# Pairwise outer-product batch norm: row 19's scale and shift spread by themselves, two pairs of its first tile done on VectorE alone, and another share for GpSimd in tiles 3 to 10

## The chip, the cores and the metric

The kernel runs on one core of one Trainium2 chip. The metric is the device time of one execution in microseconds (us); lower is better. Below, ACT is ScalarE, DVE is VectorE, POOL is GpSimd, PE is TensorE and SP is SyncE, as in the profile. SP only issues DMAs here.

## What is computed

There are 1024 samples, each with two tables of 39 rows of 16 numbers, `r_xi` and `r_xj`. For each of the 741 pairs (row r, column c < r) the kernel forms the 16x16 outer product of `xj[r]` and `xi[c]`, normalises each pair over all samples and all 256 elements, applies gamma and beta, and multiplies by a 16x16 weight.

```python
rows, cols = np.tril_indices(39, k=-1)
cross = xj[:, rows, :, None] * xi[:, cols, None, :]          # 1024 x 741 x 16 x 16
mean = jnp.mean(cross, axis=(0, 2, 3), keepdims=True)
var = jnp.mean(jnp.square(cross - mean), axis=(0, 2, 3), keepdims=True)
normed = (cross - mean) * jax.lax.rsqrt(var + 1e-5)
normed = normed * gamma[None, :, None, None] + beta[None, :, None, None]
out = normed[:, :, None, :, :] * W[None, None, :, :, :]      # 1024 x 1 x 741 x 16 x 16, f32
```

The inputs are 5 MB, the output is 777 MB. All arithmetic is f32.

## The kernel before

**Statistics first.** The 1024 samples lie as 128 partitions x 8 (index `t`). The means and variances of all pairs come from sums and small matmuls over the inputs, never from the products. This takes the first 33 us. At its end `stq` holds, for a table of 39x39 pairs, a scale s and a shift t. A matmul for each row against `pick` (line 473) spreads the s and t of that row to all 128 partitions, into PSUM. `ROW_GROUPS` (line 32) says which rows are spread together and which PSUM bank they go to: row 19 is group 0, in a bank of its own; row 20 is group 1 and rows 15 to 18 are group 2, and these two share a bank. `apply(group)` (lines 486 to 493, on DVE) multiplies in gamma and beta and leaves s and t in `st_sb`. From then on a pair is one affine step and one multiplication by the weight W.

**Tiles.** A tile is one row r with two of the eight `t` (T = 2), so r pairs of 2x256 elements, which is 0.26 MB a pair over the 128 partitions. The list of tiles begins with row 19 four times (tiles n = 0 to 3), then goes on with rows 20 and 18 in turn (n = 4 to 11), then 21 and 17, and so on. Counted from one, as in the words of the change, tiles 3 to 10 are n = 2 to 9. The output tile lies in `y_sb`, a ring which holds about four tiles; a tile's place is free again when the store of the tile that was there has landed.

**A tile from n = 1 on** goes through these steps, all written out in program order for each engine:

- `scale_xi(n)` (line 166): POOL writes `xs`, the xi rows times s. There are two buffers for `xs`, so `scale_xi(n + 2)` has to wait until ACT and POOL have finished `products(n)`.
- `products(n)` (lines 144 and 146): 2 x 16 instructions, one for each `t` and each i, which multiply `xs` by one element of xj. ACT does i < `split`, POOL the others: POOL has `POOL_I_FIRST` = 6 of 16 for n = 1 and 2, and `POOL_I` = 4 later on.
- `finish(n)`: y = (y + t) x W. DVE does it in one instruction for each pair (line 277). POOL does the last pairs of the tile, with one instruction for each pair (line 263) and one multiplication by W for all of them (line 266); their number is `int(r * 0.13 + 0.5)`, which is 2 for rows 18 and 19 and 3 for row 20.
- `store` (line 208): SP issues one DMA for each piece. The pieces of the first eight tiles are in `FIRST_PIECES`; for n = 2 they end at pairs 4, 11 and 19, for n = 3 at 9 and 19. From n = 8 to the tiles of row 24 a tile is one piece. SP issues in program order, so a piece that is not ready holds those behind it.

In the loop, POOL's order is `scale_xi(n + 2)`, its part of `finish(n)`, its part of `products(n + 1)`. DVE's is `finish(n)`, then an `apply` at n = 2, 4, 8, 16 and 24.

**Tile n = 0** is different. Its products are made without s while the statistics are still being computed (`raw_products`). When `apply(0)` is done, `affine` does y = y x s + t for each pair, the even pairs on ACT (line 221) and the odd ones on POOL (line 223), and `weigh` (line 231) multiplies a piece by W on DVE and stores it. The pieces end at pairs 2, 5, 9, 14 and 19. DVE's order is `apply(0)`, `apply(1)`, `weigh(0)`, `finish(1)`. POOL's order is five of its pairs, `scale_xi(1)`, the other four, `products(1)`, `scale_xi(2)`, and then the loop.

**Tile n = 1** (`RAW`) is finished separately for each of its two `t`, 19 pairs each, with pieces ending at pairs 4, 9, 14 and 19.

Of the kernel before, what the change touches and what calls it, by code (L numbers as in the profile page):

```python
# [9 lines left out]
ALU = mybir.AluOpType  # L10
# [6 lines left out]

ONE, LONG = 24, 33
FIRST_PIECES = (
    (0, 2, 5, 9, 14, 19), (0, 4, 9, 14, 19), (0, 4, 11, 19), (0, 9, 19), (0, 10, 20), (0, 9, 18), (0, 10, 20), (0, 9, 18)  # L20
)


POOL_I, POOL_I_LONG, POOL_I_FIRST = 4, 5, 6
POOL_SHARE, POOL_PAIRS_LONG = 0.13, 8

LOADS = (1, 2, 3, 4, 6, 8)

SHORT = 4


ROW_GROUPS = (
    (19, 20, 0, None), (20, 21, 1, None), (15, 19, 1, 2), (21, 25, 2, 4), (1, 15, 2, 8), (25, 32, 3, 16), (32, 39, 4, 24)
)


@with_exitstack
def tile_pair_outer_batchnorm(
# [15 lines left out]
    nc = tc.nc  # L54
    P = nc.NUM_PARTITIONS
    NB, F, E = xi.shape
# [8 lines left out]
    mid = (F - 1) // 2  # L65
    tiles = [(mid, t0, t0 // T * half // 2) for t0 in range(0, NT, T)]
# [8 lines left out]
    RAW = 1  # L75
# [58 lines left out]
    def view(n):  # L134
        r, _, u = tiles[n]
        return y_sb[:, u : u + T * r, :].rearrange("p (t n) e -> p t n e", t=T)

    def product(n, engine, t, i, src):

        r, t0, _ = tiles[n]  # L140
        y = view(n).rearrange("p t n (i j) -> p t n i j", j=E)[:, t, :, i, :]
        scale = xj_sb[:, t0 + t, r, i : i + 1]
        if engine is nc.scalar:
            nc.scalar.activation(y, src, AF.Copy, scale=scale)  # L144
        else:
            engine.tensor_scalar(y, src, scale, 1.0, ALU.mult, ALU.mult)  # L146
# [13 lines left out]
    def scale_xi(n):  # L160
        r, t0, _ = tiles[n]
        if r <= SHORT:
            return
        n0 = first[r]
        xs = scaled.tile([P, T, r, E], F32, tag="xs", name=f"xs_{r}_{t0}")
        nc.gpsimd.tensor_tensor(  # L166
            xs,
            xi_sb[:, t0 : t0 + T, 0:r, :],
            s_sb[:, :, n0 : n0 + r, :].to_broadcast([P, T, r, E]),
            ALU.mult,  # L170
        )
        xs_of[n] = xs

    def products(n):

        r, t0, _ = tiles[n]
        if r <= SHORT:
            xs = scaled_short.tile([P, T, r, E], F32, tag="xs_short", name=f"xs_{r}_{t0}")
            nc.vector.tensor_tensor(  # L179
                xs,  # L180
                xi_sb[:, t0 : t0 + T, 0:r, :],
                s_short[:, first[r] : first[r] + r]
                .unsqueeze(1)
                .unsqueeze(3)
                .to_broadcast([P, T, r, E]),
                ALU.mult,
            )
            for t in range(T):
                nc.vector.tensor_tensor(  # L189
                    view(n)[:, t].rearrange("p n (i j) -> p n i j", j=E),  # L190
                    xs[:, t].unsqueeze(2).to_broadcast([P, r, E, E]),
                    xj_short[:, t0 + t, r - 1 : r, :].unsqueeze(3).to_broadcast([P, r, E, E]),
                    ALU.mult,
                )
            return
        xs = xs_of.pop(n)
        split = E - (POOL_I_FIRST if n < 3 else POOL_I_LONG if tiles[n][0] > LONG else POOL_I)
        for t in range(T):
            for i in range(E):
                product(n, nc.scalar if i < split else nc.gpsimd, t, i, xs[:, t])  # L200
# [9 lines left out]
                view(n)[:, t : t + step, c0:c1, :].rearrange("p t n e -> p t (n e)"),  # L210
            )

    def affine(n, pairs):

        r = tiles[n][0]
        y = view(n)
        for c in pairs:
            s_c = st_sb[:, 0, first[r] + c : first[r] + c + 1]
            t_c = t_sb[:, first[r] + c : first[r] + c + 1]
            if c % 2 == 0:  # L220
                nc.scalar.activation(y[:, :, c, :], y[:, :, c, :], AF.Identity, bias=t_c, scale=s_c)  # L221
            else:
                nc.gpsimd.tensor_scalar(  # L223
                    y[:, :, c, :], y[:, :, c, :], s_c, t_c, ALU.mult, ALU.add
                )

    def weigh(n):

        y = view(n)
        for c0, c1 in zip(bounds(n), bounds(n)[1:]):  # L230
            nc.vector.tensor_tensor(  # L231
                y[:, :, c0:c1, :],
                y[:, :, c0:c1, :],
                w_dve.unsqueeze(1).to_broadcast([P, T, c1 - c0, EE]),
                ALU.mult,
            )
            store(n, c0, c1)

    def bounds(n):
        if n < len(FIRST_PIECES):  # L240
            return FIRST_PIECES[n]
        r = tiles[n][0]
        pieces = 1 + (r > ONE)
        return tuple(q * r // pieces for q in range(pieces + 1))

    def finish(n):


        r = tiles[n][0]
        n0 = first[r]  # L250
        y = view(n)
        long = r > LONG
        p1 = r // 2 if long else r
        p0 = p1 - (POOL_PAIRS_LONG if long else int(r * POOL_SHARE + 0.5) if r > SHORT else 0)
        step = POOL_PAIRS_LONG // 2 if long else r
        for c0 in range(p0, p1, step):
            c1 = min(c0 + step, p1)
            for c in range(c0, c1):
                t_c = t_sb[:, n0 + c : n0 + c + 1]
                if long:  # L260
                    nc.scalar.activation(y[:, :, c, :], y[:, :, c, :], AF.Identity, bias=t_c)  # L261
                else:
                    nc.gpsimd.tensor_scalar(  # L263
                        y[:, :, c, :], y[:, :, c, :], t_c, 1.0, ALU.add, ALU.mult
                    )
            nc.gpsimd.tensor_tensor(  # L266
                y[:, :, c0:c1, :],
                y[:, :, c0:c1, :],
                w_sb.unsqueeze(1).to_broadcast([P, T, c1 - c0, EE]),
                ALU.mult,  # L270
            )

        size = 1 if n == RAW else T
        for t in range(0, T, size):
            for c0, c1 in zip(bounds(n), bounds(n)[1:]):
                for c in [*range(c0, min(c1, p0)), *range(max(c0, p1), c1)]:
                    stt(  # L277
                        y[:, t : t + size, c, :],
                        y[:, t : t + size, c, :],
                        t_sb[:, n0 + c : n0 + c + 1],  # L280
                        w_dve.to_broadcast([P, size, EE]),
                        ALU.add,
                        ALU.mult,
                    )
                store(n, c0, c1, t, t + size)

    with tc.manual_schedule():
# [176 lines left out]

        spread_of = []
        used = [0] * len(ps_st)
        for r0, r1, bank, _ in ROW_GROUPS:
            n0, n1 = first[r0], first[r1 - 1] + r1 - 1
            at = used[bank]
            used[bank] = at + 2 * (n1 - n0)  # L470
            ps = ps_st[bank][:, at : used[bank]].rearrange("p (x n) -> p x n", x=2)
            for r in range(r0, r1):
                nc.tensor.matmul(  # L473
                    ps[:, :, first[r] - n0 : first[r] - n0 + r],
                    pick[:, r, :],
                    stq[:, :, 0:r],
                    start=True,
                    stop=True,
                )
            spread_of.append((ps, n0, n1))  # L480
            if r0 == 1:
                s_short = ps[:, 0]

        def apply(group):
            ps, n0, n1 = spread_of[group]
            nc.vector.tensor_mul(ps[:, 1], ps[:, 1], st_sb[:, 0, n0:n1])
            if n0 == 0:

                nc.vector.tensor_mul(ps[:, 0], ps[:, 0], st_sb[:, 0, n0:n1])
                nc.vector.tensor_copy(st_sb[:, 0, n0:n1], ps[:, 0])  # L490
            else:
                nc.vector.tensor_mul(st_sb[:, 0, n0:n1], ps[:, 0], st_sb[:, 0, n0:n1])
            nc.vector.tensor_add(st_sb[:, 1, n0:n1], ps[:, 1], st_sb[:, 1, n0:n1])

        apply(0)
        apply(1)

        affine(0, range(0, 11))
        scale_xi(1)
        affine(0, range(11, mid))  # L500
        weigh(0)
        products(1)
        scale_xi(2)

        for n in range(1, len(tiles)):
            if n + 2 < len(tiles):
                scale_xi(n + 2)
            finish(n)
            for group, (_, _, _, tile_of) in enumerate(ROW_GROUPS):
                if n == tile_of:  # L510
                    apply(group)
            if n + 1 < len(tiles):
                products(n + 1)
            if n == 32:
                nc.scalar.copy(xj_short, xj_sb[:, :, 1 : SHORT + 1, :])

# [27 lines left out]
```

## Time and profile before

| what | value |
|---|---|
| time, median of 4 runs | 1883.93 us (1883.58 to 1884.62) |
| the profiled execution: its own time | 1883.58 us |
| the profiled execution: span from first to last instruction | 1881.9 us |
| DVE, ACT, POOL busy | 92%, 87%, 81% of the span |
| output written | 776.99 MB |
| DMA queue of the stores (q1), share of the 16 DMA engines' span | 98.2% |

Times inside the execution are counted from the first instruction. The difference of 1.7 us between the span and the execution's own time lies outside the span. A row of the timeline merges like instructions that follow each other on one engine: start, duration, engine, line, result and operands, and how many; in square brackets stands the idle time of the engine before it and what ended it. A row of the windows view gives, for one stretch of the span, the busy time of each engine, then the granted TensorE clock, the mean busy share of the 16 DMA engines and the rate that they moved.

### The profile page before, as it was taken

To read this page: it belongs to the slowest core of one execution; us is meant where nothing else is said; L and a number is where in the kernel's file an instruction comes from. 1 tells how busy PE (TensorE), PEld (TensorE's weight loads), DVE (VectorE), ACT (ScalarE), POOL (GpSimd) and SP (SyncE) were. 2 spreads that over 40 slices of the span, in tenths; PEclk is the share of its full clock that TensorE was granted. 3 is DMA by queue.
4 is the path that set the end of the run, shared out by engine and by line. 5 is a ranking of instruction groups with operands and counts; after the bars stand their busy time and mean duration, and the time that the engine had idled before them with its cause. 6 is when DMAs were issued, how large, how long until landed. Compare 5 with 4: busy or idle time off the path is not lost. (4 is left out here: it accounts for less than half of the span.)

```text
span 1881.9 us, 9653 instructions
## 1 busy us (share of the span) xinstructions
PE 26.0 (1%) x130; PEld 23.3 (1%) x130; DVE 1721.9 (92%) x2627; ACT 1642.8 (87%) x3415; POOL 1524.6 (81%) x1744
## 2 busy tenths in 40 slices
PE   5000000000000000000000000000000000000000
PEld 4000000000000000000000000000000000000000
DVE  7999999998989898989898989898999999988885
ACT  8998989898989798989898989898988888888883
POOL 8998878787888787878787878787888787777873
DMA  5999999999999999999999999999999999999999
GB/s 197 374 412 427 427 430 426 431 425 425 425 427 424 427 423 424 425 424 424 426 424 423 425 426 423 418 424 423 420 422 425 423 423 426 419 423 414 425 418 410
DMA packets 63722, 783.63 MB, mean 416 GB/s; under 512 B 4768, under 2 KB 6176, under 8 KB 16800
## 3 DMA queue, kind: packets, MB, share of 16 engines
q1 hardware_dynamic: 62352, 779.72, 98.2%
q10 hardware_dynamic: 1296, 3.29, 0.5%
q14 instruction: 73, 0.60, 0.1%
q8 instruction: 1, 0.02, 0.0%
HBM read 6.00 MB, written 776.99 MB: 416 GB/s over the span
## 5 line engine op out<-in xcount | busy, mean ns | idle before, releaser
L277 DVE SCALAR_TENSOR_TENSOR y_sb<-y_sb,st_sb,w_dve 128x512 f32<-128x512 f32 (+1 forms) x2516 | 1654.2, 737 | 131.6 <-issue 118.3
L144 ACT ACTIVATE y_sb<-xs,xj_sb 128x288 f32<-128x288 f32 (+21 forms) x3192 | 1510.0, 568 | 195.2 <-DMA out_dram<-y_sb 168.7
L146 POOL TENSOR_SCALAR y_sb<-xs,xj_sb 128x384 f32<-128x384 f32 (+27 forms) x1128 | 605.7, 560 | 44.3 <-DMA out_dram<-y_sb 25.4
L266 POOL TENSOR_TENSOR y_sb<-y_sb,w_sb 128x2048 f32<-128x2048 f32 (+3 forms) x155 | 511.8, 3308 | 104.0 <-ACT y_sb L261 94.4
L166 POOL TENSOR_TENSOR xs<-xi_sb,st_sb 128x640 f32<-128x640 f32 (+33 forms) x135 | 184.0, 1363 | 177.6 <-ACT y_sb L144 172.8
L263 POOL TENSOR_SCALAR y_sb<-y_sb,st_sb 128x512 f32<-128x512 f32 x286 | 193.5, 692 | 0.1
L261 ACT ACTIVATE y_sb<-y_sb,st_sb 128x512 f32<-128x512 f32 x160 | 100.2, 708 | 1.9
L189 DVE TENSOR_TENSOR y_sb<-xs,ps 128x1024 f32<-128x1024 f32 (+3 forms) x32 | 24.8, 817 | 0.6
L473 PE MATMUL ps<-y_sb 39*128 39x38 f32 (+37 forms) x76 | 16.5, 398 | 2.8 <-DVE y_sb L461 2.8
L473 PEld LDWEIGHTS ps<-y_sb 39*128 39x128 f32 x76 | 16.3, 330 | 3.1 <-DVE y_sb L461 3.1
L339 ACT ACTIVATE y_sb<-y_sb 128x1248 f32<-128x1248 f32 x8 | 9.9, 1244 | 2.8 <-POOL y_sb L328 2.5
L344 DVE TENSOR_REDUCE y_sb<-y_sb 128x78 f32<-128x1248 f32 x8 | 11.2, 1445 | 0.4 <-ACT y_sb L339 0.4
L144 ACT ACTIVATE y_sb<-xi_sb,xj_sb 128x304 f32<-128x304 f32 x24 | 11.4, 537 | 0.0
L328 POOL TENSOR_TENSOR y_sb<-xi_sb,y_sb 128x1248 f32<-128x1248 f32 x4 | 9.2, 2323 | 2.2 <-ACT y_sb L377 2.2
L231 DVE TENSOR_TENSOR y_sb<-y_sb,w_dve 128x2560 f32<-128x2560 f32 (+3 forms) x5 | 10.5, 2170 | 0.0
L318 DVE TENSOR_REDUCE y_sb<-xi_sb 128x39 f32<-128x624 f32 (+1 forms) x6 | 6.1, 1011 | 3.9 <-DMA xi_sb<-in_r_xi_dram 3.9
L328 POOL TENSOR_TENSOR y_sb<-xj_sb,y_sb 128x1248 f32<-128x1248 f32 x4 | 9.2, 2317 | 0.0
L223 POOL TENSOR_SCALAR y_sb<-y_sb,st_sb 128x512 f32<-128x512 f32 x9 | 6.8, 766 | 2.1 <-ACT y_sb L144 2.1
L364 PE MATMUL ps<-y_sb 128*39 128x79 f32 x48 | 8.1, 340 | 15.2 <-DVE y_sb L344 15.1
L221 ACT ACTIVATE y_sb<-y_sb,st_sb 128x512 f32<-128x512 f32 x10 | 7.2, 800 | 0.2 <-ACT y_sb L144 0.2
L318 DVE TENSOR_REDUCE y_sb<-xj_sb 128x39 f32<-128x624 f32 (+1 forms) x6 | 6.1, 1014 | 0.6 <-DMA xj_sb<-in_r_xj_dram 0.6
L364 PEld LDWEIGHTS ps<-y_sb 128*39 128x39 f32 x48 | 5.8, 177 | 17.3 <-DVE y_sb L344 10.6
(58 smaller groups left out, 33.6 us busy)
## 6 DMA issues: line engine op xcount, KB each, us to landing
out_dram<-y_sb SPq DMA_DIRECT2D x25, 2304.0 KB, 14.6
out_dram<-y_sb SPq DMA_DIRECT2D x12, 4352.0 KB, 15.4
out_dram<-y_sb SPq DMA_DIRECT2D x12, 4096.0 KB, 16.3
out_dram<-y_sb SPq DMA_DIRECT2D x10, 4608.0 KB, 14.7
out_dram<-y_sb SPq DMA_DIRECT2D x12, 3840.0 KB, 17.5
out_dram<-y_sb SPq DMA_DIRECT2D x21, 2048.0 KB, 17.0
out_dram<-y_sb SPq DMA_DIRECT2D x12, 3584.0 KB, 18.1
out_dram<-y_sb SPq DMA_DIRECT2D x12, 3328.0 KB, 18.1
```

What stands on the lines that cost most here:

```text
L144: nc.scalar.activation(y, src, AF.Copy, scale=scale)
L146: engine.tensor_scalar(y, src, scale, 1.0, ALU.mult, ALU.mult)
L166: nc.gpsimd.tensor_tensor(xs, xi_sb[:, t0 : t0 + T, 0:r, :], s_sb[:, :, n0 : n0 + r, :].to_broadcast([P, T, r, E]), ALU.mult,)
L189: nc.vector.tensor_tensor(view(n)[:, t].rearrange("p n (i j) -> p n i j", j=E), xs[:, t].unsqueeze(2).to_broadcast([P, r, E, E]), xj_short ...
L261: nc.scalar.activation(y[:, :, c, :], y[:, :, c, :], AF.Identity, bias=t_c)
L263: nc.gpsimd.tensor_scalar(y[:, :, c, :], y[:, :, c, :], t_c, 1.0, ALU.add, ALU.mult)
L266: nc.gpsimd.tensor_tensor(y[:, :, c0:c1, :], y[:, :, c0:c1, :], w_sb.unsqueeze(1).to_broadcast([P, T, c1 - c0, EE]), ALU.mult,)
L277: stt(y[:, t : t + size, c, :], y[:, t : t + size, c, :], t_sb[:, n0 + c : n0 + c + 1], w_dve.to_broadcast([P, size, EE]), ALU.add, ALU.mult,)
L318: nc.vector.tensor_reduce(total[:, t0:t1, part(x)], sources[x][:, t0:t1], AX.X, ALU.add)
L328: nc.gpsimd.tensor_tensor(devs[n % 7], sources[x][:, t0 : t0 + T], shift[:, x : x + 1, :].unsqueeze(3).to_broadcast([P, T, F, E]), ALU.sub ...
L364: nc.tensor.matmul(ps_g[acc][0:F, 0 : 2 * F + 1], lhs, fb[:, t], start=t == 0, stop=t == NT - 1)
L473: nc.tensor.matmul(ps[:, :, first[r] - n0 : first[r] - n0 + r], pick[:, r, :], stq[:, :, 0:r], start=True, stop=True,)
```

## The change

- Only row 19's spread is issued before `apply(0)`. The spreads of the other groups come later in the program, after `weigh(0)`, and `apply(1)` with them. On PE the order of the matmuls is unchanged.
- In tile 0, pairs 0 and 1 (`OWN` = 2) get their affine step on DVE, inside `weigh`, ahead of the piece that they belong to. ACT and POOL begin with pairs 2 and 3, and ACT has nine pairs instead of ten, POOL eight instead of nine.
- Tile 0's pieces now end at pairs 1, 3, 6, 10, 14 and 19: six instead of five, the first of a single pair.
- `POOL_I_FIRST` becomes (6, 6, 5): in `products(2)` POOL has 5 of 16 and ACT 11. (The entry for n = 0 is not used.)
- In `finish(n)` for n = 2 to 9 POOL has three pairs. That is one more than before for n = 2, 3, 5, 7 and 9 (rows 19 and 18) and the same as before for row 20.

```diff
-    (0, 2, 5, 9, 14, 19), (0, 4, 9, 14, 19), (0, 4, 11, 19), (0, 9, 19), ...
+    (0, 1, 3, 6, 10, 14, 19), (0, 4, 9, 14, 19), (0, 4, 11, 19), (0, 9, 19), ...
-POOL_I, POOL_I_LONG, POOL_I_FIRST = 4, 5, 6
-POOL_SHARE, POOL_PAIRS_LONG = 0.13, 8
+POOL_I, POOL_I_LONG, POOL_I_FIRST = 4, 5, (6, 6, 5)
+POOL_SHARE, POOL_PAIRS_LONG, POOL_PAIRS_FIRST = 0.13, 8, 3
-SHORT = 4
+SHORT, OWN = 4, 2
...
-        split = E - (POOL_I_FIRST if n < 3 else POOL_I_LONG if tiles[n][0] > LONG else POOL_I)
+        split = E - (POOL_I_FIRST[n] if n < 3 else POOL_I_LONG if tiles[n][0] > LONG else POOL_I)
...
-    def affine(n, pairs):
+    def affine(n, pairs, engines=(nc.scalar, nc.gpsimd)):
...
-            if c % 2 == 0:
+            engine = engines[c % len(engines)]
+            if engine is nc.scalar:
                 nc.scalar.activation(y[:, :, c, :], y[:, :, c, :], AF.Identity, bias=t_c, scale=s_c)
             else:
-                nc.gpsimd.tensor_scalar(
-                    y[:, :, c, :], y[:, :, c, :], s_c, t_c, ALU.mult, ALU.add
-                )
+                engine.tensor_scalar(y[:, :, c, :], y[:, :, c, :], s_c, t_c, ALU.mult, ALU.add)
 
     def weigh(n):
...
         for c0, c1 in zip(bounds(n), bounds(n)[1:]):
+            affine(n, range(c0, min(c1, OWN)), (nc.vector,))
             nc.vector.tensor_tensor(
...
-        p0 = p1 - (POOL_PAIRS_LONG if long else int(r * POOL_SHARE + 0.5) if r > SHORT else 0)
+        if long:
+            share = POOL_PAIRS_LONG
+        elif RAW < n < 10:
+            share = POOL_PAIRS_FIRST
+        else:
+            share = int(r * POOL_SHARE + 0.5) if r > SHORT else 0
+        p0 = p1 - share
...
+        spread(0)
         apply(0)
+
+        affine(0, range(OWN, 12))
+        scale_xi(1)
+        affine(0, range(12, mid))
+        weigh(0)
+        for group in range(1, len(ROW_GROUPS)):
+            spread(group)
+        s_short = spread_of[SHORT_GROUP][0][:, 0]
         apply(1)
-
-        affine(0, range(0, 11))
-        scale_xi(1)
-        affine(0, range(11, mid))
-        weigh(0)
         products(1)
         scale_xi(2)
```

More of the change, by code (lines that the diff above doesn't have):

```diff
@@ L19 @@
 FIRST_PIECES = (
-    (0, 2, 5, 9, 14, 19), (0, 4, 9, 14, 19), (0, 4, 11, 19), (0, 9, 19), (0, 10, 20), (0, 9, 18), (0, 10, 20), (0, 9, 18)
+    (0, 1, 3, 6, 10, 14, 19), (0, 4, 9, 14, 19), (0, 4, 11, 19), (0, 9, 19), (0, 10, 20), (0, 9, 18), (0, 10, 20), (0, 9, 18)
 )
-POOL_I, POOL_I_LONG, POOL_I_FIRST = 4, 5, 6
-POOL_SHARE, POOL_PAIRS_LONG = 0.13, 8
+POOL_I, POOL_I_LONG, POOL_I_FIRST = 4, 5, (6, 6, 5)
+POOL_SHARE, POOL_PAIRS_LONG, POOL_PAIRS_FIRST = 0.13, 8, 3
 LOADS = (1, 2, 3, 4, 6, 8)
-SHORT = 4
+SHORT, OWN = 4, 2
 ROW_GROUPS = (
@@ L34 @@
 )
+SHORT_GROUP = 4
 @with_exitstack
@@ L466, in tile_pair_outer_batchnorm, with spread @@
         used = [0] * len(ps_st)
-        for r0, r1, bank, _ in ROW_GROUPS:
+        def spread(group):
+            r0, r1, bank, _ = ROW_GROUPS[group]
             n0, n1 = first[r0], first[r1 - 1] + r1 - 1
@@ L480, in tile_pair_outer_batchnorm @@
             spread_of.append((ps, n0, n1))
-            if r0 == 1:
-                s_short = ps[:, 0]
         def apply(group):
@@ L486, in apply @@
             nc.vector.tensor_mul(ps[:, 1], ps[:, 1], st_sb[:, 0, n0:n1])
-            if n0 == 0:
+            if group == SHORT_GROUP:
                 nc.vector.tensor_mul(ps[:, 0], ps[:, 0], st_sb[:, 0, n0:n1])
```

## The prediction

> **What bounds the kernel now.** First the page's DMA rows: from the third slice on the 16 DMA engines are 90% busy or more at about 425 GB/s. 777 MB at that rate take nearly the whole span, so the time is: when the stores begin, plus their length, plus the stretches in which the DMA engines have nothing to move.
>
> ```profile
> DMA  5999999999999999999999999999999999999999
> q1 hardware_dynamic: 62352, 779.72, 98.2%
> ```
>
> Second, the windows view (last two columns: DMA share, GB/s) finds those stretches.
>
> ```profile
> 38.00:39.00 1.00, 1.00 (x6) 1.00 (x7) 1.00 (x1) 1.00 (x3) 1.00 (x2) 1.00 0.58 207
> 55.00:57.00 2.00, 0.00 (x0) 0.00 (x0) 2.00 (x7) 2.00 (x6) 2.00 (x5) 1.00 0.81 325
> 64.20:65.20 1.00, 0.00 (x0) 0.00 (x0) 1.00 (x2) 1.00 (x4) 1.00 (x1) 1.00 0.01 4
> 67.80:69.70 1.90, 0.00 (x0) 0.00 (x0) 1.90 (x4) 1.90 (x6) 1.90 (x5) 1.00 0.05 19
> 79.20:80.20 1.00, 0.00 (x0) 0.00 (x0) 1.00 (x2) 1.00 (x3) 1.00 (x3) 1.00 0.00 0
> 80.20:139.20 59.00, 0.00 (x0) 0.00 (x0) 58.97 (x93) 59.00 (x136) 57.20 (x74) 1.00 1.01 422
> 139.20:140.70 1.50, 0.00 (x0) 0.00 (x0) 1.43 (x6) 1.50 (x5) 1.50 (x4) 1.00 0.11 43
> 200.00:1881.00 1681.00, 0.00 (x0) 0.00 (x0) 1533.26 (x2330) 1460.06 (x3012) 1348.71 (x1521) 1.00 1.00 424
> ```
>
> After the stores begin at 38.4, idle times are 0.4 (55 to 57), 1.0, 1.8, 1.0 and, at 139.2, 1.3 us, 5.5 in all. After 140.7 the queue stays fed. Meanwhile DVE, ACT and POOL are all full: compute is what the DMA waits for until 140.7, and not after it.
>
> Third, the timeline says which engine that is.
>
> ```profile
> 33.74 0.18 DVE L486 TENSOR_TENSOR ps<-ps,st_sb 128x19 f32<-128x19 f32 x1 [0.73 <-PE ps L473]
> 35.87 0.19 DVE L486 TENSOR_TENSOR ps<-ps,st_sb 128x20 f32<-128x20 f32 x1 [1.65 <-PE ps L473]
> 36.27 10.53 DVE L231 TENSOR_TENSOR y_sb<-y_sb,w_dve 128x1024 f32<-128x1024 f32 x5
> 46.73 13.40 DVE L277 SCALAR_TENSOR_TENSOR y_sb<-y_sb,st_sb,w_dve 128x256 f32<-128x256 f32 x34
> 61.43 11.28 DVE L277 SCALAR_TENSOR_TENSOR y_sb<-y_sb,st_sb,w_dve 128x512 f32<-128x512 f32 x17 [1.30 <-POOL y_sb L146]
> 34.38 7.16 ACT L221 ACTIVATE y_sb<-y_sb,st_sb 128x512 f32<-128x512 f32 x10 [0.17 <-ACT y_sb L144]
> 50.47 1.23 POOL L166 TENSOR_TENSOR xs<-xi_sb,st_sb 128x608 f32<-128x608 f32 x1 [0.95 <-ACT y_sb L144]
> 55.45 5.94 POOL L146 TENSOR_SCALAR y_sb<-xs,xj_sb 128x304 f32<-128x304 f32 x12
> 73.29 1.17 POOL L166 TENSOR_TENSOR xs<-xi_sb,st_sb 128x576 f32<-128x576 f32 x1 [2.81 <-ACT y_sb L144]
> 85.74 3.44 POOL L266 TENSOR_TENSOR y_sb<-y_sb,w_sb 128x1536 f32<-128x1536 f32 x1
> 64.30 4.87 SPq L208 DMA_DIRECT2D out_dram<-y_sb  x2
> 139.83 0.37 SPq L208 DMA_DIRECT2D out_dram<-y_sb  x1
> ```
>
> `apply(1)` holds DVE 1.65 us before its first weighing: rows 20 and 15 to 18 share a bank. At 61.43 DVE waits for POOL's half of tile 2. A store's data begin 0.9 us after its issue (64.30 to 65.2; 139.83 to 140.7). POOL at 73.29 really waits for row 18's scale, which `apply(2)` leaves at 73.25; ACT had long been done.
>
> **The change, step by step.** *Tile 0, DVE.* `apply(0)` ends at 34.22; the 1.65 us wait is gone, since `apply(1)` now follows `weigh(0)` and the matmuls are done by then. DVE's `affine` is an instruction that this trace does not show. The nearest row is DVE's own line 277 on 128x512: 11.28 / 17 = 0.66 us. Its smallest rows (0.17) are the floor; the ceiling is 0.75, one line 277 alone, plus up to 0.76 for the second one if it must wait for a POOL `affine` (POOL has one every 0.75 there). Two of them: 0.34 to 2.26; I take 1.32. Line 231 took 1.21 for two pairs and 1.74 for three, so 0.67 for one: pair 0 is weighed at 34.3 + 0.66 + 0.67 = 35.65, stored at 35.7 instead of 37.51. First store 1.8 us earlier. All of `weigh`: before 36.27 to 46.73; now 34.3 + 1.32 + 10.46 + 0.1 (one more instruction) = 46.2, with `apply(1)` (0.4) 46.6. `finish(1)` thus begins 0.1 earlier and, at 13.40, ends at 60.0. The ACT and POOL pairs that `weigh` needs are all there earlier, so they cost nothing.
>
> Here the Trainium skill's VectorE: DVE Perf Modes, section "The perf-mode tier table", gives f32 `tensor_scalar` in SBUF two elements a cycle; an estimate from its clock and its fixed 150 cycles is 0.42 us, and by it the sum would gain 0.25 more. Its SBUF — State Buffer, section "SBUF: two separate sides", speaks against the change: such an instruction and a GpSimd one block each other, because the port pair is an exclusive lock. No row before shows this; the wait it would bring is inside my ceiling.
>
> *Tile 1 and 2, ACT and POOL.* ACT has one `affine` less: 7.16 / 10, so 0.71 earlier. It then frees `xs` 0.71 earlier, and POOL's 50.47 becomes 49.76 (POOL's own chain, one `affine` of 0.75 shorter, has 0.95 of slack there, which covers a lock). POOL's `products(2)` begins at 54.74 and has 10 instead of 12 instructions of 5.94 / 12 = 0.495: done at 59.7. ACT has 22 instead of 20 at 0.44: 59.0 - 0.71 + 0.88 + 0.1 = 59.3. So `finish(2)` begins at 60.0, set by DVE, not at 61.43.
>
> *Tile 2 on DVE.* 16 pairs instead of 17: 60.0 + 16 x 0.66 + 0.54 (`apply(2)`) = 71.05, was 73.16. POOL's third pair (0.68 + 1.1) lies beside this: 59.75 + 1.28 + 2.03 + 0.08 + 3.44 + 3.96 = 70.55, still ahead. ACT: 0.17 later than before, 69.8, ahead too. Tile 3's first piece was issued 6.15 after its `finish` began (79.31); now 77.2, data at 78.1 instead of 80.2. Is the queue empty by then? Tile 2's second piece, issued 7.35 after 60.0, starts moving at 68.25, and the two pieces took 9.5 (69.7 to 79.2): 77.75. Yes. So by 80 the lead is 2.1 us. The first store's 1.8 is not added: it is spent in longer idle times before 69.
>
> *Tiles 3 to 9.* POOL, let go by `apply(2)` at 71.2, needs for each tile a scale (1.17 or 1.28), three pairs (2.03 + 0.08 + 3.44) and products (4.08 or 3.87), 10.8: `products(4)` to `products(8)` end at 82.0, 92.8, 103.7, 114.5, 125.3. DVE with 16, 17, 15, 17, 15 pairs of 0.661 would be ready at 81.6, 93.9, 103.8, 115.0, 124.95: the two run level. `finish(8)` begins at 125.35 and its store goes out 17 x 0.661 + 0.15 later at 136.75 (before 139.83), data at 137.65. ACT reaches the same place at 122.7. The pieces of tiles 3 to 7 came out no slower than 422 GB/s before, and come out earlier here, so the queue is fed: it runs dry at 139.35 - 2.1 = 137.2, where before it stood 1.3 us until 140.7. Tile 8 begins 140.7 - 137.65 = **3.0 us earlier**.
>
> *After that* ACT waits for landings (`ACT y_sb L144 <- DMA out_dram<-y_sb`, 168.7 us in the waits), so everything moves with the DMA: 3.0 stays. The extra store is 0.37 of SP's issue time, before 40, and hides.
>
> **Sum.** 1883.58 - 3.0 = 1880.6 for a run like the profiled one, which is 0.35 under the median of the runs; for a median, 1880.9. With two `affine` of 0.17, POOL sets 59.75: 0.25 more gained. With 2.26 for both, DVE comes 0.95 later: 2.05 gained. Own range 1880.3 to 1882.1 with the runs' spread.
>
> **Rivals.** *All idle times from 64 on close* (5.1 us): 1878.8. For it: three engines get lighter or start earlier. Against it: tile 2's second piece can't leave before 67.35, and the stores ahead of it are through by 66.4.
>
> *POOL becomes the bound and the kernel gets slower.* Place: tiles 2 to 9, where POOL and DVE run level and every tile has three POOL pairs. POOL's chain from 59.75 to 125.3 is 65.6 us of back-to-back instructions; if they run 5% slower than these rows, the 3.1 us between 136.75 and 139.83 are gone. That is the point from which it decides. POOL's 128x512 `tensor_scalar` is 0.75 in line 223 and 0.68 in line 263, so 10% exists between rows: 6.6 - 3.1 = 3.5 slower, and tiles 10 and 11 behind it add about 1: 1888. Against it: line 266's cost for three pairs, 3.44, is measured on row 20, four times alike.
>
> *The lead is given back*, because a later stretch is bound by compute after all, or the parts don't act as said: 1883.6. Against it: DMA share 1.00 from 200 on.
>
> **How the numbers follow.** A measurement of this kernel tells about 0.2% (3.8 us) from no change, so faster means below 1880.2, and my forecast lies just inside "same". Forecast 0.74, of which a fifth falls under 1880.2 (0.14); all idle closes 0.08; given back 0.09; POOL bound 0.09, nearly all beyond 0.2%. Faster 0.22, same 0.70, slower 0.08. The range takes in the own range and three fifths of the way to the two near rivals: 1879.3 to 1883.0.
>
> **What would show it.** DVE's line 231 beginning near 35 with no wait for PE ahead of it; first data near 36.6; `finish(2)` at 60.0; the idle at 67.8 still there and about as long; data of tile 3 at 78; no idle left at 139; POOL's line 266 at 3.44 in tiles 2 to 9. I am wrong if `finish(3)` begins later than 71.5, if POOL is waited for by DVE for over 1 us in tiles 3 to 9, or if the DMA share after 200 falls.

## The result, and the profile after

The changed kernel takes 1881.55 us (median of 41 runs, 1880.99 to 1882.19) against 1883.92 us before (61 runs): 2.37 us less, a ratio of 0.9987 with a 95% interval of 0.9983 to 0.9992. The interval leaves out "no change", and the gain lies inside the 0.2% that the prediction called "same". The forecast was 3.0 us less, 1880.9, with a range from 1879.3 to 1883.0. The profiled execution took 1881.39 us, its span is 1879.7 us (before 1883.58 and 1881.9). In the new file `finish` on DVE is line 284, `weigh` 232, `affine` on DVE and POOL 225, POOL's weighing 273 and the stores 209.

First the windows of the changed kernel: behind its first store, the stretches in which its DMA still stands, and the later ones (last columns: DMA share, GB/s):

```profile
37.00:39.00 2.00, 2.00 (x12) 2.00 (x11) 2.00 (x2) 2.00 (x4) 2.00 (x4) 1.00 0.41 137
63.85:64.46 0.61, 0.00 (x0) 0.00 (x0) 0.61 (x2) 0.61 (x2) 0.61 (x1) 1.00 0.02 7
67.20:68.95 1.75, 0.00 (x0) 0.00 (x0) 1.75 (x4) 1.75 (x5) 1.75 (x4) 1.00 0.01 4
78.50:78.80 0.30, 0.00 (x0) 0.00 (x0) 0.30 (x1) 0.30 (x2) 0.30 (x2) 1.00 0.00 0
137.00:139.00 2.00, 0.00 (x0) 0.00 (x0) 1.93 (x7) 2.00 (x6) 2.00 (x3) 1.00 1.05 437
200.00:1878.00 1678.00, 0.00 (x0) 0.00 (x0) 1530.76 (x2326) 1457.51 (x3006) 1346.19 (x1518) 1.00 1.00 424
```

The idle at 64 shrank from 1.0 to 0.6 us and the one at 79 from 1.0 to 0.3; the one at 68 is as long as it was (1.75), and the 1.3 us at 139 are gone. Tile 3's data start at 78.8 instead of 80.2. From 200 on the rate is what it was, 424 GB/s.

The timeline of the changed kernel gives the engines' side:

```profile
33.86 0.18 DVE L493 TENSOR_TENSOR ps<-ps,st_sb 128x19 f32<-128x19 f32 x1 [0.73 <-PE ps L482]
34.48 0.56 DVE L225 TENSOR_SCALAR y_sb<-y_sb,st_sb 128x512 f32<-128x512 f32 x1
35.07 0.69 DVE L232 TENSOR_TENSOR y_sb<-y_sb,w_dve 128x512 f32<-128x512 f32 x1
35.68 0.95 DVE L225 TENSOR_SCALAR y_sb<-y_sb,st_sb 128x512 f32<-128x512 f32 x1
36.73 10.01 DVE L232 TENSOR_TENSOR y_sb<-y_sb,w_dve 128x1024 f32<-128x1024 f32 x5
47.38 2.04 DVE L284 SCALAR_TENSOR_TENSOR y_sb<-y_sb,st_sb,w_dve 128x256 f32<-128x256 f32 x5 [0.24 <-issue]
71.77 10.61 DVE L284 SCALAR_TENSOR_TENSOR y_sb<-y_sb,st_sb,w_dve 128x512 f32<-128x512 f32 x16
125.83 11.28 DVE L284 SCALAR_TENSOR_TENSOR y_sb<-y_sb,st_sb,w_dve 128x512 f32<-128x512 f32 x17 [0.32 <-POOL y_sb L147]
35.91 2.46 SPq L209 DMA_DIRECT2D out_dram<-y_sb  x2
137.26 0.37 SPq L209 DMA_DIRECT2D out_dram<-y_sb  x1
```

The wait for PE ahead of the weighing is gone, and the first store leaves at 35.91 instead of 37.51. But the two affine steps of one shape take 0.56 and 0.95 us, and `finish(1)` begins at 47.38, later than before (46.73). Even so `finish(3)` begins at 71.77, which is 1.4 us earlier, `finish(8)` begins at 125.83, and tile 8's store leaves at 137.26 instead of 139.83.

### The profile page after: what moved, and what is told of

Read it like the earlier page. It is cut to its first block, busy times and chain, and to the rows that moved or that the text cites. A ratio compares the mean times of both kernels' runs of the same rounds, so it can differ in the third digit from the quotient of the medians.

```text
span 1879.7 us, 9660 instructions
## 1 busy us (share of the span) xinstructions
PE 26.0 (1%) x130; PEld 23.3 (1%) x130; DVE 1720.4 (92%) x2625; ACT 1642.9 (87%) x3416; POOL 1532.0 (82%) x1746
## 5 line engine op out<-in xcount | busy, mean ns | idle before, releaser
L145 ACT ACTIVATE y_sb<-xs,xj_sb 128x288 f32<-128x288 f32 (+20 forms) x3194 | 1510.7, 565 | 192.8 <-DMA out_dram<-y_sb 166.2
L147 POOL TENSOR_SCALAR y_sb<-xs,xj_sb 128x416 f32<-128x416 f32 (+29 forms) x1126 | 604.8, 561 | 41.1 <-DMA out_dram<-y_sb 27.9
L273 POOL TENSOR_TENSOR y_sb<-y_sb,w_sb 128x2048 f32<-128x2048 f32 (+3 forms) x155 | 517.2, 3343 | 103.8 <-ACT y_sb L268 94.3
L232 DVE TENSOR_TENSOR y_sb<-y_sb,w_dve 128x2048 f32<-128x2048 f32 (+4 forms) x6 | 10.7, 1836 | 0.1
```

The source lines that it names most:

```text
L273: nc.gpsimd.tensor_tensor(y[:, :, c0:c1, :], y[:, :, c0:c1, :], w_sb.unsqueeze(1).to_broadcast([P, T, c1 - c0, EE]), ALU.mult,)
```

## The experiments

Two theories. **A**: the gain is made by the new shares, through the time at which `finish(3)` begins and through tile 8's store; what happens in tile 0 is used up in longer idle times before 69. **B**: the gain comes from the earlier first store. Then: what did VectorE's two pairs cost, and what else does the early DMA wait for? All times below are medians; the change has 41 runs, each other kernel of the table 11, and the kernel before stood at 1883.86 to 1883.92 beside them. Two of the intervals reach just past 1: tile 0's part alone and the three pairs alone. For these the traces have to say what was gained. "Lead" below is how much earlier a kernel has moved the same bytes than the kernel before, counted from the packets of the stores in the two traces.

| kernel | us | against before | 95% interval of the ratio |
|---|---|---|---|
| the change | 1881.55 | -2.37 | 0.9983 to 0.9992 |
| tile 0's part alone | 1882.96 | -0.96 | 0.9987 to 1.0004 |
| shares alone | 1881.32 | -2.60 | 0.9978 to 0.9996 |
| change, one pair on VectorE | 1880.73 | -3.19 | 0.9974 to 0.9992 |
| change, no pair on VectorE | 1881.39 | -2.53 | 0.9978 to 0.9996 |
| three POOL pairs alone | 1882.29 | -1.62 | 0.9983 to 1.0001 |
| change, finer pieces | 1881.21 | -2.70 | 0.9977 to 0.9994 |
| one pair, finer pieces | 1880.40 | -3.51 | 0.9972 to 0.9990 |
| change, tiles 8 to 11 in halves | 1881.90 | -1.96 | 0.9981 to 0.9998 |
| one pair, pieces cut only where the DMA waited | 1879.80 | -4.06 | 0.9969 to 0.9987 |

**1. Tile 0's part alone, and the shares alone.** The first undoes the shares in the changed kernel, the second puts them alone into the kernel before.

```diff
-POOL_I, POOL_I_LONG, POOL_I_FIRST = 4, 5, (6, 6, 5)
+POOL_I, POOL_I_LONG, POOL_I_FIRST = 4, 5, (6, 6, 6)
...
-        elif RAW < n < 10:
+        elif False:
```

> The changed kernel with the shares of GpSimd put back (6 of 16 products in tile 2; 2 pairs for rows 18 and 19): only tile 0 and the order of the spreads differ from the kernel before. Theory A (the shares bring the gain, by the time at which tile 3's finish begins): GpSimd's products of tile 2 end at 54.9 + 12 x 0.495 = 60.8, finish(2) begins at 60.85 instead of 61.43, finish(3) at 72.6 instead of 73.16, tile 3's data at 79.6 instead of 80.2, the idle at 139 stays: 0.6 us faster, 1883.3. Theory B (the store that leaves 1.6 us earlier brings the gain): 1.6 to 2.4 us faster, 1881.5 to 1882.3, first data at 36.8.

```diff
-        split = E - (POOL_I_FIRST if n < 3 else ...
+        split = E - ((6, 6, 5)[n] if n < 3 else ...
...
+        elif RAW < n < 10:
+            share = 3
...
```

> The kernel before with the new shares alone (5 of 16 products for GpSimd in tile 2; three pairs in tiles n = 2 to 9); tile 0 as before, first store at 37.5. Theory A: GpSimd's products of tile 2 end at 55.45 + 4.95 = 60.4, finish(2) begins at 60.45 (after: 60.70), finish(3) at 71.5 (after: 71.77), tile 3's data at 78.55 instead of 80.2, tile 8's store goes out at 137.2: 2.5 us faster, 1881.4, as much as the whole change. Theory B: 0 to 0.8 us faster, 1883.1 to 1883.9.

The timeline (`finish(3)`) and the windows of tile 0's part alone, and then the same two of the shares alone:

```profile
72.73 7.98 DVE L284 SCALAR_TENSOR_TENSOR y_sb<-y_sb,st_sb,w_dve 128x512 f32<-128x512 f32 x12
134.00:141.00 7.00, 0.00 (x0) 0.00 (x0) 6.93 (x14) 7.00 (x17) 6.92 (x10) 1.00 0.83 347
```

```profile
60.63 10.62 DVE L283 SCALAR_TENSOR_TENSOR y_sb<-y_sb,st_sb,w_dve 128x512 f32<-128x512 f32 x16 [0.34 <-POOL y_sb L146]
71.71 1.40 DVE L283 SCALAR_TENSOR_TENSOR y_sb<-y_sb,st_sb,w_dve 128x512 f32<-128x512 f32 x2
134.00:141.00 7.00, 0.00 (x0) 0.00 (x0) 6.93 (x14) 7.00 (x16) 6.83 (x11) 1.00 1.01 422
```

Theory A holds. With the first store still at 37.68, the shares alone gain 2.60 us, as much as the whole change. Tile 0's part alone, with its earlier store, gains 0.96, nearer to A's 0.6 than to B's 1.6; the idle at 139 is still there (share 0.83). Its trace is clearer than its time: its lead is 0.4 us at 80 and still 0.4 at 150, which is what `finish(3)` gained (72.73 instead of 73.16), and not the 1.5 us by which its first store left earlier. The two parts don't add (0.96 and 2.60 make 2.37): both move the same instant, the start of `finish(3)`, 71.71 with the shares alone and 71.77 with both.

**2. How many pairs on VectorE.**

```diff
-SHORT, OWN = 4, 2
+SHORT, OWN = 4, 1
```

> The changed kernel with one pair on VectorE instead of two (OWN = 1); pair 1 goes back to GpSimd, the pieces stay 1, 3, 6, 10, 14, 19. If VectorE's second affine (0.95 us, and 0.10 before the next weighing) sets finish(1) and with it everything to tile 3: finish(1) begins at 46.3 instead of 47.4, finish(2) at 60.0 (then set by GpSimd's products), finish(3) at 71.1 instead of 71.8, tile 3's data at 78.1, 0.6 to 0.7 us faster than the changed kernel: about 1880.9. If the second affine is covered by other waits: as the changed kernel, 1881.5.

```diff
-    (0, 1, 3, 6, 10, 14, 19), (0, 4, 9, 14, 19), ...
+    (0, 2, 5, 9, 14, 19), (0, 4, 9, 14, 19), ...
-SHORT, OWN = 4, 2
+SHORT, OWN = 4, 0
...
-        affine(0, range(OWN, 12))
+        affine(0, range(0, 11))
         scale_xi(1)
-        affine(0, range(12, mid))
+        affine(0, range(11, mid))
```

> The changed kernel with no pair on VectorE: affine steps and pieces of tile 0 as in the kernel before, row 19 still spread alone and apply(1) behind weigh(0), new shares. VectorE weighs from 35.4 (when ScalarE's and GpSimd's first pairs are there) instead of 36.27 before; first store at 36.65. Theory A: ScalarE and GpSimd have their pairs back, GpSimd's products of tile 2 end at 60.5, finish(2) begins at 60.6, finish(3) at 71.6: as the changed kernel within 0.3 us, 1881.4. If instead the two pairs on VectorE are worth their 0.7 us of relief to ScalarE: 0.7 us slower than the changed kernel, 1882.2.

One pair is best: 0.82 us faster than the changed kernel, and no pair at all is as good as two (that kernel also has the old pieces of tile 0). It differs from the shares alone (1881.32) only by the place of the spreads and of `apply(1)`, so with the new shares the spread of row 19 by itself gained nothing that these runs can tell. Timeline of the kernel with one pair, then of the one with none:

```profile
46.74 1.65 DVE L284 SCALAR_TENSOR_TENSOR y_sb<-y_sb,st_sb,w_dve 128x256 f32<-128x256 f32 x4
71.12 2.06 DVE L284 SCALAR_TENSOR_TENSOR y_sb<-y_sb,st_sb,w_dve 128x512 f32<-128x512 f32 x3
```

```profile
35.38 1.22 DVE L232 TENSOR_TENSOR y_sb<-y_sb,w_dve 128x1024 f32<-128x1024 f32 x1 [1.08 <-POOL y_sb L225]
71.63 2.05 DVE L284 SCALAR_TENSOR_TENSOR y_sb<-y_sb,st_sb,w_dve 128x512 f32<-128x512 f32 x3
```

With one pair `finish(3)` begins 0.65 earlier than in the changed kernel, and the time falls by 0.82. Its start of `finish(1)` was expected at 46.3 and is 46.74: DVE now waits twice for POOL's pairs in tile 0, 0.25 and 0.26. With no pair DVE is free at 34.3 but waits 1.08 for POOL's first pair and twice more later (0.19 and 0.33), and `finish(1)` begins at 46.93, no earlier than before.

**3. Why the second affine took 0.95.** GpSimd is held until both of VectorE's affine are done, by giving it pair 1's weighing as its first task, which VectorE's `weigh` then leaves out. It was profiled once, and that is its only time (1882.16; POOL starts over a microsecond later in it).

```diff
-            affine(n, range(c0, min(c1, OWN)), (nc.vector,))
+            d0 = 2 if c0 == 1 else c0
...
+        affine(0, range(0, OWN), (nc.vector,))
+        y0 = view(0)
+        nc.gpsimd.tensor_tensor(
+            y0[:, :, 1:2, :], y0[:, :, 1:2, :],
+            w_sb.unsqueeze(1).to_broadcast([P, T, 1, EE]), ALU.mult,
+        )
         affine(0, range(OWN, 12))
```

> The changed kernel with both affine steps of VectorE issued back to back ahead of the weighing, and GpSimd held until they are done: its first instruction in tile 0 becomes the weighing of pair 1, which needs VectorE's second affine. No GpSimd instruction runs beside either affine. If a GpSimd instruction and VectorE's affine shut each other out: both VectorE affine take the same 0.35 to 0.56 us (in the changed kernel 0.56 and 0.95), and all GpSimd affine take 0.75 to 0.77 (there 1.00 and 0.93 for those beside VectorE's). If the 0.95 has another cause, such as the pair or its place behind a weighing: the second affine stays near 0.95, and GpSimd's first affine near 1.0.

The line's instructions with shortest, median and longest duration in ns, in the changed kernel and then in this one:

```profile
L225 POOL TENSOR_SCALAR y_sb<-y_sb,st_sb x8: 753/765/1002, 34.6 to 41.4; 128x512 f32<-128x512 f32 x8
L225 DVE TENSOR_SCALAR y_sb<-y_sb,st_sb x2: 560/756/952, 34.5 to 35.7; 128x512 f32<-128x512 f32 x2
```

```profile
L225 POOL TENSOR_SCALAR y_sb<-y_sb,st_sb x8: 757/764/767, 37.0 to 43.4; 128x512 f32<-128x512 f32 x8
L225 DVE TENSOR_SCALAR y_sb<-y_sb,st_sb x2: 540/544/547, 34.5 to 34.9; 128x512 f32<-128x512 f32 x2
```

Apart from each other, every DVE affine takes 0.54 and every POOL affine 0.76. Side by side the second DVE affine takes 0.41 more and POOL's slowest 0.24 more. This run also takes the weighing from between the two affine, so by itself it doesn't rule out that the place behind a weighing made VectorE's second one longer. The starts in the changed kernel speak for GpSimd: in each of the three overlaps the instruction that began second is the longer one. POOL's first began at 34.59, after VectorE's first (34.48), and took 1.00 while VectorE's took 0.56; VectorE's second began at 35.68, after POOL's second (35.59), and took 0.95 while POOL's took 0.75; POOL's third began at 36.34, before that one had ended, and took 0.93. POOL's other five took 0.76.

**4. The three pairs alone.** In the kernel before:

```diff
...
+        elif RAW < n < 10:
+            share = 3
...
```

> The kernel before with three GpSimd pairs in tiles n = 2 to 9 and nothing else; products of tile 2 stay at 6 of 16. Theory A: finish(2) begins at 61.4 as before, finish(3) at 72.5 (0.66 earlier), tile 3's data at 79.5, tiles 3, 5 and 7 each 0.66 shorter, the 1.3 us of idle at 139 gone: 1.9 us faster, 1882.0, and so 0.6 us less than with the 5 of 16 as well. If tile 2's products matter for the DMA's lead alone and the idle at 139 stays: 0.7 us faster, 1883.2.

1882.29, 1.62 us less: near A's 1.9, far from 0.7. So 5 of 16 products in tile 2, which the shares alone have as well (2.60), are worth the other 1.0. Its timeline and windows:

```profile
61.65 10.62 DVE L283 SCALAR_TENSOR_TENSOR y_sb<-y_sb,st_sb,w_dve 128x512 f32<-128x512 f32 x16 [1.30 <-POOL y_sb L146]
134.00:141.00 7.00, 0.00 (x0) 0.00 (x0) 6.93 (x15) 7.00 (x16) 6.83 (x13) 1.00 1.04 433
```

DVE's wait of 1.30 for POOL's products stands as before, and the idle at 139 is gone: that one is closed by the pairs, not by tile 2. The lead agrees with the time: 0.4 us at 80, 1.6 at 141.

**5. Finer pieces.** In the changed kernel, and then with one pair on VectorE:

```diff
-    ..., (0, 4, 11, 19), (0, 9, 19), (0, 10, 20), (0, 9, 18), (0, 10, 20), (0, 9, 18)
+    ..., (0, 4, 8, 13, 19), (0, 4, 9, 14, 19), (0, 5, 10, 20), (0, 9, 18), (0, 10, 20), (0, 9, 18),
+    (0, 10, 20), (0, 9, 18), (0, 10, 20), (0, 9, 18)
```

> The changed kernel with finer pieces: tile 2 ends at 4, 8, 13, 19 (was 4, 11, 19), tile 3 at 4, 9, 14, 19 (was 9, 19), tile 4 at 5, 10, 20, and tiles n = 8 to 11 in two halves. Same work on every engine. If the idle of 2.6 us at 64, 67 and 79 is the size of the piece that the DMA waits for: about 1 us of it stays (64 and the second and third piece of tile 2), 1.5 us faster than the changed kernel, 1880.0. If what counts is only when finish(3) begins: no difference, 1881.5.

> The kernel with one pair on VectorE (OWN = 1) and these finer pieces. One pair alone gave 0.8 us over the changed kernel. If the two gains add: 2.0 to 2.3 us faster than the changed kernel, 1879.3 to 1879.5. If the DMA is by then fed by nothing but VectorE's pace: no more than one of them, 1880 to 1880.7.

The first gained 0.34 instead of 1.5, a miss, and 0.34 is hardly clear of the spread (1880.73 to 1881.64 against 1880.99 to 1882.19). The second gained 0.33 over one pair alone. That lies in the range given for VectorE's pace as the limit, but by the medians the two gains did add (0.82 and 0.34 over the changed kernel, 1.15 together), and only the one of the pieces was small. In the trace of the first the idle of 2.6 us had shrunk to 1.1 and the lead was there at tile 8 (3.6 us at 141), and then part of it went (2.9 at 188). The next kernel asks where, with only the halves of tiles 8 to 11:

```diff
...
+    (0, 10, 20), (0, 9, 18), (0, 10, 20), (0, 9, 18)
```

> The changed kernel with tiles n = 8 to 11 stored in two halves and nothing else; its DMA queue was never empty there. In the kernel with finer pieces the DMA moved 421 GB/s from 138 to 186 us, in the changed kernel 430. If the shorter stores themselves move slower: 48 x 9 / 425 = 1.0 us at most, 0.6 to 1.0 us slower than the changed kernel, 1882.2 to 1882.5, rate again about 421. If that rate was only the queue's state: 1881.5, rate about 430.

Windows of the changed kernel, of the one with finer pieces, and of the one with halves only:

```profile
138.00:186.00 48.00, 0.00 (x0) 0.00 (x0) 48.00 (x74) 43.00 (x98) 46.26 (x58) 1.00 1.01 430
```

```profile
138.00:186.00 48.00, 0.00 (x0) 0.00 (x0) 48.00 (x74) 48.00 (x110) 47.25 (x60) 1.00 1.01 421
```

```profile
138.00:186.00 48.00, 0.00 (x0) 0.00 (x0) 48.00 (x74) 47.85 (x109) 47.25 (x61) 1.00 1.01 423
```

Same DMA share, 1.01, but 2% less moved: stores of 9 and 10 pairs are slower than stores of 18 and 20. A packet of 10240 bytes took 389 ns, one of 20480 took 766 (medians of this stretch): two small ones take 12 ns more. It cost 0.35 us against the changed kernel, less than the 0.6 expected, but in the trace the halves did cost 0.7: the lead fell from 2.9 at 141 to 2.2 at 188, where the changed kernel has 2.5 at both. It stood 0.4 higher at 141, 0.2 of which it already had at 80. So the pieces were cut only where the DMA had waited:

```diff
-    ..., (0, 4, 11, 19), (0, 9, 19), (0, 10, 20), (0, 9, 18), (0, 10, 20), (0, 9, 18)
+    ..., (0, 4, 8, 13, 19), (0, 6, 12, 19), (0, 9, 20), (0, 9, 18), (0, 10, 20), (0, 9, 18),
+    (0, 10, 20)
...
-SHORT, OWN = 4, 2
+SHORT, OWN = 4, 1
```

> One pair on VectorE, and pieces cut only where the DMA waited: tile 2 at 4, 8, 13, 19, tile 3 at 6, 12, 19, tile 4 at 9, 20, tile 8 at 10, 20; all others as in the changed kernel. If shorter stores cost as said and the idle at 64 to 79 stays closed: 0.5 to 0.7 us faster than the kernel with all the finer pieces and one pair (1880.4): 1879.7 to 1879.9, 4.1 us under the kernel before. If the shorter stores cost nothing: 1880.4 or, with new idle, up to 1880.8.

1879.80, as expected: 1.75 us under the changed kernel, 4.06 under the kernel before (ratio 0.9978, 0.9969 to 0.9987), and the best of all. Of the three stretches of idle the first is down to 0.3 us, the second to 0.5 and the third is closed, by the shares in its windows:

```profile
63.00:64.00 1.00, 0.00 (x0) 0.00 (x0) 1.00 (x2) 1.00 (x3) 0.92 (x2) 1.00 0.72 280
67.00:70.00 3.00, 0.00 (x0) 0.00 (x0) 3.00 (x5) 3.00 (x8) 3.00 (x7) 1.00 0.82 327
77.00:80.00 3.00, 0.00 (x0) 0.00 (x0) 3.00 (x6) 3.00 (x8) 3.00 (x5) 1.00 1.05 426
```

## Why the prediction was right, and where it was not

**What bounds the kernel: right.** Every gain went with closing or shortening an idle stretch of the DMA before 141; the one loss against the changed kernel, with tiles 8 to 11 in halves, came from the rate. From 200 on 424 GB/s stayed 424.

**The first store's 1.8 us is spent, not gained: right**, shown by experiment 1. It left 1.6 us earlier, and the shares without it gained just as much. The place was not the stretches that the prediction had listed, which did not get longer (0.6 and 1.75 us at 64 and 68, before 1.0 and 1.8). The first store now carries one pair and is soon moved; behind it the DMA waits for the second store, which leaves at 37.98 (share 0.41 from 37 to 39). At 50 us 0.3 of the lead was left.

**Tile 0 on DVE: the mis-sized term.** Two affine were put at 0.66 each, so that `finish(1)` would begin at 46.6; it began at 47.38, 0.78 later. One of the signs that the prediction had set for being wrong, `finish(3)` later than 71.5, thus came true: it began at 71.77. The 0.78 in order: the statistics ended 0.12 later in this execution; the first affine began 0.06 later after `apply(0)` than assumed; from its start to the weighing of pairs 1 and 2 it was 2.25 us instead of 1.99; and from `apply(1)` to `finish(1)` 0.72 instead of 0.40, of which 0.24 is an idle time that the profile calls "issue". The 0.26 come from the second affine: 0.95 against the 0.54 that experiment 3 measured by itself; the first affine and the weighing were a little shorter than assumed. Without the second, in the kernel with one pair, the idle "issue" is gone as well, and the time is 0.82 us shorter. What that idle is was not settled: it stands in all four kernels with two pairs on VectorE inside `weigh`, and in none of the others, that of experiment 3 included.

The bound that the prediction set (0.75 plus up to 0.76 of waiting for a POOL instruction) held the 0.95. It had let the Trainium skill's SBUF — State Buffer, section "SBUF: two separate sides", in as a possible wait only. That section says that of a VectorE instruction in a two-port mode and a GpSimd instruction the one that starts first keeps the other out for its whole length. The runs agree that the second one is held: 0.95 against 0.54 on DVE, 1.00 and 0.93 against 0.76 on POOL. They don't show a wait for the whole length: the three grew by 0.41, 0.24 and 0.17 us, while the other instruction still had 0.67, 0.44 and 0.29 to run, in the same order. The same skill's VectorE: DVE Perf Modes gave an estimate of 0.42 for the affine; alone it is 0.54, still less than the 0.66 taken from line 277.

**Tile 2: right but for what it inherits.** POOL's `products(2)` was done at 59.82, in time, and DVE set `finish(2)`, at 60.70; `finish(3)` was forecast at 71.05 and came at 71.77, 0.72 late, nearly the whole delay of `finish(1)`. Tile 3's data came at 78.8, forecast 78.1. The idle at 67.8 stayed about as long, as forecast.

**Tiles 3 to 9: right.** POOL and DVE run level: DVE waits twice for POOL, 0.30 at `finish(4)` and 0.32 at `finish(8)`, which begins at 125.83 against the forecast 125.35. POOL's weighing of three pairs stayed at 3.44 in all eight tiles (shortest, median and longest in ns), so the rival in which POOL's instructions get slower and it becomes the bound did not come about:

```profile
L273 POOL TENSOR_TENSOR y_sb<-y_sb,w_sb x8: 3439/3442/3453, 63.3 to 139.9; 128x1536 f32<-128x1536 f32 x8
```

**The sum.** Tile 8's store left at 137.26 against the forecast 136.75, so it was 2.57 earlier than before instead of 3.08; the spans differ by 2.2 and the medians by 2.37. Of the 0.63 us that are missing from the 3.0, 0.51 are thus missing at tile 8 already. They come from the late `finish(1)`: in the kernel with one pair, where it begins 0.64 earlier, the lead at 141 is 3.1, in the changed kernel 2.5. The rest goes late: in these two executions the lead of the changed kernel is mostly between 2.3 and 2.6 up to 1460 us and 2.2 to 2.3 from 1700 on. Why stays open; no experiment was made for it.

## What to carry to other kernels

Where a queue of transfers is the bound, look for the last stretch in which it stands empty and ask what has to be ready at its end: whatever else happens before that, such as an earlier first store, is only waited for there. A step moved to another engine is priced with what runs beside it, and each further step anew: here one pair on VectorE was better than none and better than two. Cut a transfer into pieces only where the queue waits for it, since elsewhere the smaller pieces cost rate.

## What the runs showed of the hardware

VectorE's f32 `tensor_scalar` with two scalars for each partition, 128x512, takes 0.54 us (0.46 from start to start), against 0.74 (0.66) for `scalar_tensor_tensor` on the same shape. When it began after a GpSimd `tensor_scalar` it took 0.95; GpSimd's, when it began after VectorE's, took 1.00 and 0.93 instead of 0.76. VectorE's weighing, which has one of its two operands in PSUM, took 1.22 for two pairs beside the same GpSimd instructions, and 1.21 in the kernel before; no run shows it for two pairs with GpSimd at rest. Stores of 9 and 10 pairs moved 421 to 423 GB/s where stores of 18 and 20 pairs moved 430, with the DMA engines equally busy.
